# An attention and sign-weight block on one core: where a division is done, and how projection work is laid between attention steps

## The chip, the cores and the metric

The kernel runs on one core of one Trainium2 chip. Such a core has a matrix engine (TensorE, PE in the profile; its weight loads are listed apart as PEld), a vector engine (VectorE, DVE), a scalar engine (ScalarE, ACT), a general engine (GpSimd, POOL) and a queue engine that only issues transfers (SyncE, SP). POOL issues transfers as well as computing. Each engine works through its own list of instructions in order; semaphores hold an instruction until what it needs is there. The metric is the device time of one execution in microseconds (us), and the median of several executions is compared.

## The reference

The input is x of shape (2, 1024, 1024): two batches of 1024 tokens of 1024 channels. After a layer norm, xn goes into two branches whose results are added to x:

```
x = x + attention(xn) + binary_linear(xn)
attention:
  q, k, v = split(clip(xn @ Wqkv.T, -8, 8))
  q, k = layer_norm(q) * w + b, layer_norm(k) * w + b     # over 1024 channels
  32 heads of 32 channels
  scores = q k^T / sqrt(32) + slope[h] * (key - query), causal
  softmax over keys, times v; then @ Wout.T
binary_linear:
  W = mean(|W_real|, axis=1) * sign(W_real);  xn @ W.T + bias
```

All inputs and outputs are float32.

## The kernel before

**Projections.** Each of q, k, v and the output projection is a product of 1024x1024 blocks done with seven half-size products instead of eight (function `seven`, in the order of `ORDER`: 11, 21, t2, t3, t4, t1, 22). One of the seven is a group: four contraction chunks into one bank of PSUM, eight matmul instructions of 512 columns in the trace (each float32 product is two passes). A pair of token tiles (256 tokens) takes seven groups. `combine` folds the seven results on DVE and ACT. q and k rows are then layer-normed and transposed by `to_channels`, and stored to DRAM. The generator `pieces` hands out all of this as small pieces in order: k, q, v of the first batch, k, q, v of the second, then the sign-weight product (`binary_linear`), then the output projection (`output`). A yield gives a planner's cost: ONE = 0.915 for one chunk of a group, SHORT = 1.03 for four matmuls of the sign-weight product, TURN = 0.55 for four transposes.

**Attention.** Work is cut into 32 blocks (batch, half of the queries `qb`, group `g` of four heads). Per block there are first scores (`first_scores`, queries on partitions, DVE takes the row maxima straight out of PSUM, L1025) and second scores (`second_scores`, keys on partitions, the maxima brought in as three bfloat16 rows, L1081; DVE adds the causal mask on diagonal tiles, L1100; ACT takes the exponential out of PSUM into `pT`, L1109). `weigh_values` multiplies `pT` by the values (L1149); POOL adds up the `pT` tiles (L1138) for the softmax denominators. `divide` brings the denominators together with eight matmuls (`den`, L1168), ACT takes ln and exp(-1 x ln) (L1176, L1177), POOL multiplies (L1182, for the very last block DVE, L1180) and issues the store to DRAM (L1183). A matrix of 128 x 512 scores per head fills one of seven PSUM banks of the pool `ps_s`; the banks are handed out in turn, so a new tile waits until the tile seven allocations back has been read.

**The order of the steps.** The loop over n (L1228) is written out by hand. Step n holds, in this order: the first scores of unit n; when a block has closed, the start of its `shifts`; when a block's values were finished in the step before, its `divide`; a first `fill`; the values of unit n-10; the second scores of unit n-9 (LAG is 9); a second `fill`. There are 144 units and so steps 0 to 154. `fill(time)` draws pieces until its planned time is used up and carries an overdraft to the next call in `left["time"]`; in one of the two fills of a step the `sides` (layer norms, transposes, sign preparation) move on too. `middle` is 81. In steps below 81 a step's free time is `share` (8.08) less what attention is planned to take: 7.03 in steps 0 to 8, 4.63 in steps 10 to 80. BEFORE = 0.4 of it goes into the first fill and 0.6 into the second. From step 81 on there is only the second fill, with `each` = 3.69 and `whole=True`, by which the call goes on until the group that it has begun is finished. After the last step, `fill(float("inf"))` runs what is left.

**Start.** `projected("k", 0)` loads and norms token tiles 0 and 1, `turn_x` transposes a tile in two halves of four 128x128 transposes, and the first group follows. The last operation of `spread` (L501) is one ACT instruction over all 1024 channels, in place.

**End.** The last two pairs of token tiles of the output projection (14 groups) need the last block's division: `output` returns None until it is done, and then a `fill` stops and its balance is set to zero.

**Queues.** SP issues the weight loads (`load_weights`, into a ring of 28 tiles), the loads of keys, queries and values (L930, L934, L943), `load_pair` (L557), `prefetch` (L844) and the residual copies (L660). POOL issues the stores of intermediate results.

Of the kernel before, what the change touches and what calls it, by code (L numbers as in the profile page):

```python
# [8 lines left out]
FP = mybir.dt.float32  # L9
FR = mybir.dt.float32r  # L10
BF = mybir.dt.bfloat16
AF = mybir.ActivationFunctionType
ALU = mybir.AluOpType
# [12 lines left out]
def parallel_block_kernel(  # L26
# [36 lines left out]
    nc = tc.nc  # L63
    B, S, D = x.shape
    P = 128
    NT = S // P
    NC = D // P
    HALF = 512
# [7 lines left out]


    ONE, SHORT, TURN = 0.915, 1.03, 0.55
    BEFORE = 0.4
    PART, FOLD, SWITCH = 0.95 / 512, 0.3 / 512, 0.1  # L80
    QK_SCALE = HEAD_DIM ** (-0.5)
    slopes = [2.0 ** (-(h + 1) * ALIBI_BIAS_MAX / N_HEADS) for h in range(N_HEADS)]
# [6 lines left out]
    work = ctx.enter_context(tc.tile_pool(name="work", bufs=2))  # L89
# [117 lines left out]
    def half(n):  # L207
        return slice(n * HALF, (n + 1) * HALF)
# [127 lines left out]
    def advance_sides():  # L336
        time = 0.0
        for s in list(sides):
            cost = next(s, None)
            if cost is None:  # L340
                sides.remove(s)
            else:
                time += cost
        return time
# [10 lines left out]
    def score_bank(name):  # L355
        return ps_s.tile([P, HALF], FP, tag="s", name=name)
# [7 lines left out]
    kd, qd, vd, od, xd = ({} for _ in range(5))  # L364
# [29 lines left out]
    held = [False]  # L394
# [88 lines left out]
    def spread(src, stats, what):  # L483

        mv = small.tile([P, 2], FP, tag="mv", name=f"mv_{what}")
        nc.vector.bn_aggr(mv, stats.rearrange("p n s -> p (n s)"))
        if what[:2] != "x0":
            yield 0.0
        rstd = small.tile([P, 1], FP, tag="rstd", name=f"rstd_{what}")
        nc.scalar.activation(rstd, mv[:, 1:2], AF.Ln, bias=eps_t)  # L490
        nc.scalar.activation(rstd, rstd, AF.Exp, scale=-0.5)
        yield 0.0

        mean, var = mv[:, 0:1], mv[:, 1:2]
        t = small.tile([P, 1], FP, tag="newton", name=f"newton_{what}")
        nc.vector.tensor_scalar(var, var, EPS, -0.5, ALU.add, ALU.mult)
        nc.vector.tensor_scalar(t, rstd, var, rstd, ALU.mult, ALU.mult)
        nc.vector.tensor_scalar(rstd, t, 1.5, rstd, ALU.add, ALU.mult)
        nc.vector.tensor_scalar(t, mean, -1.0, rstd, ALU.mult, ALU.mult)
        yield 0.0  # L500
        nc.scalar.activation(src, src, AF.Identity, bias=t, scale=rstd)  # L501

    def transposed(src, c0, what):
        ps = ps_s.tile([P, 4, P], FP, tag="s", name=f"tr_{what}_{c0}")
# [312 lines left out]
    blocks = [(b, qb, g) for b in range(B) for qb in range(NQB) for g in range(NC)]  # L817
# [75 lines left out]
    def pieces():  # L893
        for b in range(B):
            yield from keys_or_queries("k", b)
            yield from keys_or_queries("q", b)
            yield from values(b)
        yield from binary_linear()
        yield from output()

    left = {"pieces": pieces(), "time": 0.0, "owed": 0.0}

    def fill(time, whole=False, sides_too=True):

        left["time"] += time
        while left["time"] > 0.0 or (whole and held[0]):
            cost = next(left["pieces"], None)
            if cost is None:  # L910
                left["time"] = 0.0
                break
            left["owed"] += 0.5
            left["time"] -= cost
            if sides_too and left["owed"] >= 1.0:
                left["owed"] -= 1.0
                left["time"] -= advance_sides()

    def fill_until(what):
        while what not in done:  # L920
            left["time"] = 0.0
            fill(0.01)
# [5 lines left out]
    def load_keys(b, qb, g):  # L928
        q = group.tile([P, HALF], FP, tag="q", name=f"qg_{b}_{qb}_{g}", bufs=6)
        nc.sync.dma_start(q, qd[b][g][:, half(qb)])  # L930
        k = []
        for n in range(qb + 1):
            k.append(group.tile([P, HALF], FP, tag="k", name=f"kg_{b}_{qb}_{g}_{n}", bufs=6))
            nc.sync.dma_start(k[n], kd[b][g][:, half(n)])  # L934
        st["q", b, qb, g], st["k", b, qb, g] = q, k
# [13 lines left out]
    def open_block(*block):  # L949
        st[("mx",) + block] = small.tile(  # L950
            [P, G, NQ], FP, tag="mx", name="mx_{}_{}_{}".format(*block), bufs=3
        )
# [210 lines left out]
    def divide(b, qb, g):  # L1163

        ps = score_bank(f"den_{b}_{g}_{qb}")
        total = st.pop(("sum", b, qb, g))
        for j in range(G):
            nc.tensor.matmul(  # L1168
                ps[32 * j : 32 * j + 32, :],
                ones,  # L1170
                total[j],
                start=True,
                stop=True,
            )
        inv = work.tile([P, HALF], FP, tag="inv", name=f"inv_{b}_{g}_{qb}", bufs=1)
        nc.scalar.activation(inv, ps, AF.Ln)  # L1176
        nc.scalar.activation(inv, inv, AF.Exp, scale=-1.0)  # L1177
        ot = st["ot", b, qb, g]
        if (b, qb, g) == blocks[-1]:
            nc.vector.tensor_tensor(ot, ot, inv, ALU.mult)  # L1180
        else:
            nc.gpsimd.tensor_tensor(ot, ot, inv, ALU.mult)  # L1182
            nc.gpsimd.dma_start(od[b][g][:, half(qb)], ot)  # L1183
        done.add(("o", b, qb, g))


# [30 lines left out]
    def short_lead(block):  # L1217

        return block[1] == 1 and block[2] == 0
# [3 lines left out]
    for n in range(3):  # L1223
        if n in opens:
            load_keys(*opens[n])
    fill(proj - AHEAD * ONE)
    chains = []
    for n in range(steps + 1):  # L1228
        if n + 3 in opens and not short_lead(opens[n + 3]):
            fill_until(("q", opens[n + 3][0]))  # L1230
            load_keys(*opens[n + 3])
        if n + 2 in weighs:
            block = weighs[n + 2]
            fill_until(("v", block[0]))
            load_values(*block)
        if n in opens:
            open_block(*opens[n])
        if n < len(first):
            first_scores(first[n])
        closing = shifts(*closes[n]) if n in closes else None  # L1240
        if closing:
            next(closing)
        m = n - LAG
        if m - 2 in ends:
            divide(*ends[m - 2])
        free = max(share - time_of(n), 0.0)
        if n < middle:
            fill(free * BEFORE, sides_too=False)
        if 0 <= m - 1 < len(second):
            weigh_values(second[m - 1], ends.get(m - 1))  # L1250
        if 0 <= m < len(second):
            second_scores(second[m])
        for c in chains:
            next(c, None)
        chains = [closing] if closing else []
        if n + 2 in opens and short_lead(opens[n + 2]):
            fill_until(("q", opens[n + 2][0]))
            load_keys(*opens[n + 2])
        if n < middle:
            fill(free * (1.0 - BEFORE))  # L1260
        else:
            fill(each, whole=True)
    fill(float("inf"))
# [51 lines left out]
```

## Time and profile before

| what | value |
|---|---|
| median of 3 executions | 1578.15 us (1576.8 to 1581.82) |
| the profiled execution | 1580.05 us, its span 1578.3 us |
| granted TensorE clock, mean | 0.992 |
| POOL: multiplication in `divide`, L1182 | 31 x 1273 ns, and 114.3 us of waiting before them |
| POOL: issue of its store, L1183 | 31 x 619 ns |
| ACT: ln out of PSUM, L1176; exp, L1177 | 32 x 601 ns; 32 x 630 ns |
| ACT: last step of the norm of x, L501 | 16 x 1269 ns |
| step of the second half with a whole group, 1365.95 to 1372.94 us | 6.99 us |

How to read it: a page of the profile gives busy time per engine and groups of instructions with their mean duration; the chain of waits and the list of waits say what ended an engine's idle time; the timeline lists instructions in order of time, with start and duration. A matmul that waits in the middle of a group shows as a group that lasts long, not as idle time of PE. So how long PE really spends on a group is read from the start of the group to the start of whatever PE does next.

### The profile page before, as it was taken

Reading aid. Unit: us, or ns where it says so; the run is one execution under the profiler, and the core shown is the slowest. Engines: PE = TensorE matmul, PEld = TensorE weight load, DVE = VectorE, ACT = ScalarE, POOL = GpSimd, SP = SyncE. Lnnn points to the kernel's source line nnn. Section 1 sums busy time; section 2 is a strip of 40 time slices with the busy share of each in tenths; the row PEclk is TensorE's granted clock in tenths of the full one; section 3 lists DMA queues with packets and bytes.
Section 4 is the critical chain, followed back from the end, with each engine's and each line's share of the span. In section 5 each row is a group of like instructions: output and inputs, shape, how many; then the busy total and the mean of one; then the engine's idle time right before and its main releaser. Section 6 shows DMA issues by size and latency. Waiting matters only on the chain.

```text
span 1578.3 us, 25307 instructions
## 1 busy us (share of the span) xinstructions
PE 1553.1 (98%) x8452; PEld 682.3 (43%) x8452; DVE 909.5 (58%) x2602; ACT 688.5 (44%) x1425; POOL 998.8 (63%) x1306
## 2 busy tenths in 40 slices
PE   7999999999999999999999999999999999999998
PEld 3444444444444434333333344555555433333343
DVE  7745353766676666666666555656555556555232
ACT  2553341114665645545542374545444434434420
POOL 4473071024675566676566599887798988778841
PEclk9999999999999999999999999999899999999999
DMA  7776364592323655558742377656565831233232
GB/s 290 295 254 261 100 206 151 185 324 74 107 95 112 224 191 182 131 129 253 249 159 94 115 250 221 140 130 136 134 147 97 225 87 39 77 81 74 57 78 53
DMA packets 116466, 244.94 MB, mean 155 GB/s; under 512 B 10544, under 2 KB 50992, under 8 KB 113008
## 3 DMA queue, kind: packets, MB, share of 16 engines
q1 hardware_dynamic: 88752, 145.01, 27.8%
q0 software_dynamic: 27584, 98.32, 24.0%
q8 instruction: 67, 1.10, 0.3%
q14 instruction: 63, 0.52, 0.1%
HBM read 155.47 MB, written 107.74 MB: 167 GB/s over the span
## 4 chain that ended last, share of the span: by engine, by line
PE 65%; DVE 1%; POOL 1%; issue 1%; ACT 1%; DMA 0%; POOLq 0%; DVEq 0%; ACTq 0%
PE s L1006 9%; PE s L1067 9%; PE o L1149 8%; PE mm_f L793 8%; PE mm_o_t L402 7%; PE mm_o L402 5%; PE mm_q_t L402 4%; PE mm_v_t L402 4%; PE mm_q L402 3%; PE mm_v L402 3%; PE den L1168 2%; PE s L1081 2%; PE mm_k_t L402 1%; PE mm_k L402 0%; PE tr_q L506 0%
## 5 line engine op out<-in xcount | busy, mean ns | idle before, releaser
L1138 POOL TENSOR_TENSOR pT<-pT,pT 128x512 f32<-128x512 f32 (+3 forms) x628 | 579.9, 983 | 101.8 <-ACT pT L1109 100.9
L1109 ACT ACTIVATE pT<-s,kpos 128x512 f32<-128x512 f32 (+3 forms) x768 | 378.2, 590 | 464.5 <-DVE s L1100 274.1
L1025 DVE CUSTOM_DVE_ANT_0 sumss<-s,rel 128x512 f32<-128x512 f32 (+2 forms) x284 | 179.1, 631 | 112.4 <-PE s L1006 79.3
L1006 PE MATMUL s<-kg,qg 32*128 32x512 f32 (+3 forms) x1536 | 197.3, 523 | 0.7 <-ACT kT L570 0.6
L1067 PE MATMUL s<-qg,kg 32*128 32x512 f32 (+3 forms) x1536 | 176.7, 525 | 1.3 <-DVE mx L1025 1.3
L1149 PE MATMUL o<-pT,vg 128*32 128x512 f32 (+3 forms) x1536 | 155.3, 499 | 0.0
L793 PE MATMUL mm_f<-sg,hl 128*128 128x512 f32 x512 | 128.6, 403 | 2.1 <-DVE mx L1025 2.1
L1006 PEld LDWEIGHTS s<-kg,qg 32*128 32x128 f32 x1536 | 80.0, 183 | 110.4 <-issue 44.8
L1100 DVE TENSOR_TENSOR s<-s,behind 128x256 f32<-128x256 f32 (+1 forms) x320 | 96.9, 371 | 48.1 <-PE s L1081 47.9
L402 PE MATMUL mm_o_t<-w_o_t,ot 128*128 128x512 f32 x256 | 116.6, 602 | 0.0
L1067 PEld LDWEIGHTS s<-qg,kg 32*128 32x128 f32 x1536 | 71.7, 185 | 101.4 <-issue 56.3
L1182 POOL TENSOR_TENSOR ot<-ot,inv 128x512 f32<-128x512 f32 x31 | 39.5, 1273 | 114.3 <-ACT inv L1177 114.3
L402 PE MATMUL mm_k_t<-w_k_t,xT 128*128 128x512 f32 x224 | 110.7, 614 | 0.5 <-DVE mx L1025 0.4
L793 PEld LDWEIGHTS mm_f<-sg,hl 128*128 128x128 f32 x512 | 94.7, 190 | 34.4 <-DVE mx L1025 10.6
L402 PE MATMUL mm_q_t<-w_q_t,xp 128*128 128x512 f32 x224 | 108.2, 605 | 0.0
L402 PE MATMUL mm_v_t<-w_v_t,xp 128*128 128x512 f32 x224 | 106.3, 606 | 0.1
L402 PE MATMUL mm_k<-w_k,xT 128*128 128x512 f32 x192 | 91.4, 616 | 0.9 <-DVE mx L1025 0.7
L402 PE MATMUL mm_v<-w_v,xp 128*128 128x512 f32 x192 | 89.6, 604 | 0.0
L1149 PEld LDWEIGHTS o<-pT,vg 128*32 128x32 f32 x1536 | 37.3, 109 | 119.1 <-issue 102.8
L402 PE MATMUL mm_q<-w_q,xp 128*128 128x512 f32 x192 | 88.7, 603 | 0.0
L402 PE MATMUL mm_o<-w_o,ot 128*128 128x512 f32 x192 | 87.5, 602 | 0.1
L1025 DVE CUSTOM_DVE_ANT_0 umss<-s,rel 128x512 f32<-128x512 f32 x100 | 69.2, 692 | 26.1 <-PE s L1006 15.3
(222 smaller groups left out, 2009.0 us busy)
## 6 DMA issues: line engine op xcount, KB each, us to landing
xp<-xd SPq DMA_DIRECT2D x16, 1792.0 KB, 8.3
kg<-kd SPq DMA_DIRECT2D x48, 256.0 KB, 5.0
vg<-vd SPq DMA_DIRECT2D x48, 256.0 KB, 7.9
wd_ot<-in_wout_t_dram POOLq DMA_DIRECT2D x11, 1024.0 KB, 9.4
xd<-xT POOLq DMA_DIRECT2D x8, 1280.0 KB, 5.3
x<-in_x_dram SPq DMA_DIRECT2D x16, 512.0 KB, 6.3
kd<-kT POOLq DMA_DIRECT2D x16, 512.0 KB, 4.1
qd<-qT POOLq DMA_DIRECT2D x16, 512.0 KB, 4.2
```

What stands on the lines that cost most here:

```text
L402: nc.tensor.matmul(ps, pr[:, FACTOR[block], c, :], W[what, block, c], start=(c == 0), stop=(c == NI - 1),)
L793: nc.tensor.matmul(ps, hl[c // NI][:, m % 2, c % NI, :].bitcast(FR), sg[n, c], start=(m == 0), stop=(m == 2 * NC - 1),)
L1006: nc.tensor.matmul(banks[j][:, c0 : c0 + n], q[r, tokens(i - block[1] * NQ)], k[r, :n], start=True, stop=True,)
L1025: nc.vector.tensor_tensor_reduce(out=sums[:, :n], in0=banks[j][:, c0 : c0 + n], in1=rel[:, o0 : o0 + n], scale=1.0, scalar=m if opened els ...
L1067: nc.tensor.matmul(banks[j][:, c0:c1], k[r, tokens(kt % NQ)], q[r, q0:], start=(c0 == 0), stop=False,)
L1081: nc.tensor.matmul(banks[j][:, c0:c1], ones_b[r, :], rows[r, q0:], start=False, stop=(c1 == HALF or (block, kt, q0) == unit[-1]),)
L1100: nc.vector.tensor_tensor(at, at, mask, ALU.add)
L1109: nc.scalar.activation(pT[:, c0:c1], banks[j][:, c0:c1], AF.Exp, bias=kpos[:, h, a : a + 1], scale=slopes[h],)
L1138: eng.tensor_tensor(part_sum, part_sum, pT[j], ALU.add)
L1149: nc.tensor.matmul(po[32 * j : 32 * j + 32, q0:], v[:, kt % NQ, 32 * j : 32 * j + 32], pT[j], start=(kt == 0), stop=(last is not None and ...
L1168: nc.tensor.matmul(ps[32 * j : 32 * j + 32, :], ones, total[j], start=True, stop=True,)
L1182: nc.gpsimd.tensor_tensor(ot, ot, inv, ALU.mult)
```

## The change

Four edits.

1. In `divide`, ln and exp work in place in the PSUM bank of `den`, the tile `inv` is gone, DVE does the multiplication in all blocks with that bank as an operand, and SP issues the store.
2. In `spread`, the last ACT instruction for token tiles 0 and 1 of the first batch is done as two instructions over 512 channels each.
3. The first fill of a step below 81 gets what is over 4.0 of the free time (LATER), and the second gets the rest, up to 4.0. In steps 10 to 80 that is 0.63 and 4.0 instead of 1.85 and 2.78.
4. A call of `fill` with `whole=True` draws at least one piece, whatever the balance.

```diff
-    BEFORE = 0.4
+    LATER = 4.0
...
-        nc.scalar.activation(src, src, AF.Identity, bias=t, scale=rstd)
+        parts = (half(0), half(1)) if what in ("x0_0", "x0_1") else (slice(0, D),)
+        for at in parts:
+            nc.scalar.activation(
+                src[:, at], src[:, at], AF.Identity, bias=t, scale=rstd
+            )
...
         left["time"] += time
-        while left["time"] > 0.0 or (whole and held[0]):
+        none = whole
+        while left["time"] > 0.0 or none or (whole and held[0]):
+            none = False
             cost = next(left["pieces"], None)
...
-        inv = work.tile([P, HALF], FP, tag="inv", name=f"inv_{b}_{g}_{qb}", bufs=1)
-        nc.scalar.activation(inv, ps, AF.Ln)
-        nc.scalar.activation(inv, inv, AF.Exp, scale=-1.0)
+        nc.scalar.activation(ps, ps, AF.Ln)
+        nc.scalar.activation(ps, ps, AF.Exp, scale=-1.0)
         ot = st["ot", b, qb, g]
-        if (b, qb, g) == blocks[-1]:
-            nc.vector.tensor_tensor(ot, ot, inv, ALU.mult)
-        else:
-            nc.gpsimd.tensor_tensor(ot, ot, inv, ALU.mult)
-            nc.gpsimd.dma_start(od[b][g][:, half(qb)], ot)
+        nc.vector.tensor_tensor(ot, ps, ot, ALU.mult)
+        if (b, qb, g) != blocks[-1]:
+            nc.sync.dma_start(od[b][g][:, half(qb)], ot)
         done.add(("o", b, qb, g))
...
         if n < middle:
-            fill(free * BEFORE, sides_too=False)
+            fill(max(free - LATER, 0.0), sides_too=False)
...
         if n < middle:
-            fill(free * (1.0 - BEFORE))
+            fill(min(free, LATER))
         else:
             fill(each, whole=True)
```

## The prediction

> **What bounds the kernel now.** I read the page first: PE is busy for 98% of the span and every other engine for 64% or less.
>
> ```profile
> span 1578.3 us, 25307 instructions
> PE 1553.1 (98%) x8452; PEld 682.3 (43%) x8452; DVE 909.5 (58%) x2602; ACT 688.5 (44%) x1425; POOL 998.8 (63%) x1306
> ```
>
> PE is the bound, so only three things can pay: PE starting sooner, waiting less, or switching less between kinds of work. Waits inside a group count as busy, so I went to the timeline next (start, duration, engine and line, operation) and measured each group from its start to the start of PE's next work. A quiet step of the second half:
>
> ```profile
> 1365.95 1.14 PE L1006 MATMUL s<-kg,qg 32*128 32x512 f32 x8
> ...
> 1369.31 3.70 PE L402 MATMUL mm_o_t<-w_o_t,ot 128*128 128x512 f32 x8
> ...
> 1372.94 1.14 PE L1006 MATMUL s<-kg,qg 32*128 32x512 f32 x8
> ```
>
> First scores take 1.07 (to 1367.02, where the values start), and no first fill exists here; 3.63 of product after the second scores is enough for the next first scores to start unheld. Now a step while the second batch's keys are projected:
>
> ```profile
> 495.58 3.03 ACT L1109 ACTIVATE pT<-s,kpos 128x384 f32<-128x384 f32 x8 [4.64 <-DVE s L1100]
> ...
> 497.75 2.03 PE L1006 MATMUL s<-kg,qg 32*128 32x512 f32 x8
> ...
> 499.71 0.70 PE L402 MATMUL mm_k_t<-w_k_t,xT 128*128 128x512 f32 x1
> ```
>
> First scores take 1.96 here, because the exponentials of the step before still hold two of the banks until 498.6; 2.7 us of product lay between. Over steps 9 to 80 the first scores are held in 27 steps, by 22.7 us in all. In the second half the worst places are steps that have no product at all:
>
> ```profile
> 1125.17 5.55 PE L1006 MATMUL s<-kg,qg 32*128 32x512 f32 x8
> ...
> 1127.76 3.03 ACT L1109 ACTIVATE pT<-s,kpos 128x256 f32<-128x256 f32 x8 [3.93 <-DVE s L1100]
> ...
> 1134.11 5.64 PE L793 MATMUL mm_f<-sg,hl 128*128 128x512 f32 x16
> ```
>
> The second scores end at 1125.17 and the next first scores follow at once; they are held for 4.4 us, and then the sixteen sign-weight matmuls, 3.85 elsewhere, take 5.57. The view of windows says why (columns: window, length, busy time of PE, PEld, DVE, ACT, POOL with counts, then the granted clock):
>
> ```profile
> 1132.00:1136.00 4.00, 4.00 (x17) 1.85 (x14) 0.89 (x4) 1.91 (x4) 1.65 (x8) 0.50 0.23 46
> ```
>
> After a hold of some 4 us the clock is halved for a while. Last, the end of attention, and two lines of the list of waits (waiter, releaser, us in total, times, longest):
>
> ```profile
> 1509.34 1.15 PE L1067 MATMUL s<-qg,kg 32*128 32x384 f32 x16
> ...
> 1514.19 1.37 DVE L1138 TENSOR_TENSOR pT<-pT,pT 128x384 f32<-128x384 f32 x5 [0.17 <-ACT pT L1109]
> ...
> 1518.90 1.06 PE L1168 MATMUL den<-pT,ones 128*32 128x512 f32 x8
> ```
>
> ```profile
> POOL ot L1182 <- ACT inv L1177: 114.3, 26, 9.8
> ...
> PEld s L1067 <- DVE mx L1025: 29.5, 51, 1.4
> ```
>
> **A product at least in each step.** From step 81 a step is granted 3.686 but a sign-weight group costs 4 x 1.03 = 4.12, so the balance falls by 0.434 a step and after 8 or 9 steps the grant doesn't lift it above zero. That gives three steps without a product: 89, 98 and 108 (second scores followed by first scores at 1052.45, 1125.17 and 1203.03). What they cost: steps 89 and 90 together take 18.05, where the same groups unheld take 3.27 + 1.07 + 0.88 + 1.40 + 0.97 + 0.33 + 3.85 = 11.8, so 6.3; step 99 takes 14.51 instead of 7.24, so 7.3; step 109 takes 9.64 instead of 8.49, so 1.1. With the edit all three get a group: **-14.7**.
>
> What is late next: three groups are used up sooner. Before, 29 sign-weight and 42 free output groups last from step 81 to 153 with three gaps (the 42nd behind the last division at 1519.9); now 71 groups fill steps 81 to 151, and steps 152 and 153 have none. There the last second scores (1509.34 in the trace, 1.29 long) are followed by their values (1.0) and the last division, whose sums DVE ends at 1515.56, 6.2 us after those scores began. PE has 2.3 of work in 6.2: a hold of 3.95, which 8.3 us of product and values covered before. Holds of 3.6 (step 90) and 4.4 (step 99) were each followed by half clock, for some 6.8 and 10.2 us by windows over them (0.56 over 1055 to 1062; 0.82, 0.50, 0.50, 0.82 from 1125 to 1141), and a shorter one near 355 by 3.4. Half of the middle one is 3.4 of lost time; ends 0 and 5.1. Together **+7.3** (4 to 9). Behind the division the sixth output group needs nothing new: the first group of the last pairs reads only channels stored long before, 3.4 us against the 3.2 that ln, exp and product took (1518.90 to 1522.09), and only the fourth chunk of the second needs the result.
>
> The Trainium skill, "TensorE: Matmul & The Clock Gate", section "What's actually happening", says that an idle window of about 3.4 us halves the clock and that about as long a busy one restores it; by that the end's half clock would cost 1.7, an estimate from that page, and the sum below would be 1547. The trace agrees on the halving, but its spells were one to three such windows long, so I stay with the row.
>
> **Length of the fills.** The total is the same (4.63 in steps 10 to 80), so the same pieces run. With 0.63 before and 4.0 after, and 0.915 a piece, the carry gives mostly one piece before and four after, and in about a third of the steps none and five, where it was two and three. The stretch from second scores to next first scores grows by 0.86 to 1.7 us. A hold can shrink by no more than itself, nor by more than the exponentials come sooner relative to it: in 17 held steps behind four row maxima (0.69 + 0.08, done some 3.9 after first scores begin) the cut by 1.2 each, or the whole where smaller, is 12.5 of 14.0; in the others, behind eight short maxima, which end 5 us or more after, the mask waits for DVE anyway, and I take half of 8.7. **-16.8**; ends -8 (the first kind alone by 0.6) and -22.7.
>
> Each run of products between attention work pays about 0.19 beside its matmuls (x6 takes 2.77, x4 1.91: 0.43 a matmul and 0.19 once). A third of some 71 steps lose one run: **-5** (-3 to -7). The cost side: second scores now come up to 1.2 us sooner after the first scores whose banks they take over. Weight loads for them already wait 29.5 us for the maxima, while PE is still busy; in the second half, with no first fill at all, second scores take 0.96, unheld. So 0, with up to +7 (0.1 a step) as upper end. The values keep the same distance to their exponentials.
>
> **Division.** POOL loses 31 x 1.27, 31 x 0.62 of issuing and 114.3 us of waiting in order, behind which stood its sums and shifts. PE waited for POOL only a little: transposes of shifts, 0.23 free, took longer by 3.7 us in the second half and 1.9 before. I take **-1** (0 to -5). DVE gets 32 x 0.69 (the row of `u_o` from PSUM, 692 ns), one of them there before. In order, the product stands behind the maxima of its step and ahead of the masks. In 24 of 30 divisions with maxima in the step exp ended before the last maximum; in the others it would hold DVE for up to 2.2, 5.5 us in all. Masks and with them exponentials come 0.7 later in those steps, mostly into slack: **+1** (0 to +10; all on the path would be 27). Ln and exp in place: no row has PSUM to PSUM; copies out of PSUM take 0.59 and exp between SBUF 0.63, so +-0.05, nothing. The bank is held until the product, 2 to 3 us longer; it is needed seven allocations on, a step later: 0.
>
> The store waits on SP for DVE's product. In 30 of 31 cases SP had issued the load ahead of it before that (0.29 late in one), so it goes out 0.9 to 4 us sooner than POOL did, and the next block's copy into `ot` (two waits, 8.8 us) gains at no cost to PE. Loads behind it on SP can no longer run ahead: up to 19 us later (queries at 864.9, used near 904, landing in 6.4; the last sign weight at 939.0 by 4.7, landed at 945.0, used at 953.9): 0.
>
> **Start.** ACT's 1.24 us instruction at 7.17 becomes two of about 0.63. The first transposes begin at 7.9 instead of 8.55, ACT's copy and the first product (10.31) come earlier by the same: **-0.55** (0 if weight loads, which PEld awaits at 13.03, take over; -0.65 at most).
>
> **Sum:** -14.7 + 7.3 - 16.8 - 5 - 1 + 1 - 0.55 = -29.75. The profiled execution took 1580.05 (span 1578.3 and 1.75 around it), so 1550.3; it stands 1.9 above the median of the three, and from the median the sum is 1548.4, say **1548**.
>
> **Rivals.** (a) The holds stay: DVE and ACT, not the place of the second scores, set when banks come free while keys are projected (DVE 70% and ACT 64% busy from 410 to 470). Against it: there DVE waits for PE before the masks (1.9 us at 495). Then 1548.4 + 16.8 = **1565**. (b) The end takes the product's gain back: 14.7 instead of 7.3 lost if the half clock comes twice: **1556**. (c) Slower: second scores are pinned by DVE's reading of the first scores' banks, so what moves behind them only turns into a wait ahead of them. If each of 71 steps loses 0.86 there and the holds stay, 1565 + 61 = **1626**; it decides at 29.75 / 71 = 0.42 a step. For it: the 29.5 us of waiting weight loads. Against it: unheld second scores in the quiet steps. (d) The least piece never acts, since all is carried anyway: 1548.4 + 14.7 - 7.3 = 1556; against it stand the three bare steps, which the carry explains to the step.
>
> **Chances.** The forecast as worked 0.58, (a) 0.17, (b) and (d) 0.10, (c) 0.09, several small losses that leave no change 0.06. Differences under 0.3% (5 us) a measurement of this kernel can't tell from none. Faster 0.85, same 0.05, slower 0.10. The range goes from 1535 (all holds gone, no half clock at the end) to 1567 (past (a)).
>
> **What would show it.** Right: no two scores without product after 1000 us; a bare stretch of some 4 us ahead of the last `den`, half clock behind it; 14 groups after that `den`, not 15; `den` and its product on DVE without long waits; first scores near 1.07 in steps 11 to 80; POOL near 960 us busy (998.8 - 39.5). Wrong: L1067 or L1081 groups that grow in steps 10 to 80, or DVE standing before its product.

## The result, and the profile after

The changed kernel takes 1575.72 us (median of 20 executions, 1569.74 to 1578.78) against 1579.56 us for the kernel before (20 executions, 1576.61 to 1583.57): a ratio of 0.997 with an interval of 0.9959 to 0.9981. It is 4 to 5 us faster (3.8 by the medians, 4.7 by the ratio); the forecast was 30, and 1575.72 lies above the range of 1535 to 1567. The profiled execution took 1578.76 us, its span 1577.0, 1.3 us less than the span before. It lies 3 us above the median, so the trace is that of one of the longer executions. A gain of this size says little about which edits worked, so the places come first.

The head of the page of the changed kernel, and from its list of groups (busy us, mean ns | idle before) the attention scores that answer to L1006 and L1067 before:

```profile
span 1577.0 us, 25397 instructions
...
PE 1554.0 (99%) x8452; PEld 684.3 (43%) x8452; DVE 928.5 (59%) x2633; ACT 687.0 (44%) x1427; POOL 939.5 (60%) x1244
...
L1073 PE MATMUL s<-qg,kg 32*128 32x512 f32 (+3 forms) x1536 | 199.9, 526 | 1.9 <-DVE mx L1031 1.7
L1012 PE MATMUL s<-kg,qg 32*128 32x512 f32 (+3 forms) x1536 | 173.0, 521 | 0.2
```

The two lines of the kernel before:

```profile
L1006 PE MATMUL s<-kg,qg 32*128 32x512 f32 (+3 forms) x1536 | 197.3, 523 | 0.7 <-ACT kT L570 0.6
L1067 PE MATMUL s<-qg,kg 32*128 32x512 f32 (+3 forms) x1536 | 176.7, 525 | 1.3 <-DVE mx L1025 1.3
```

First scores (L1012) last 24.3 us less, second scores (L1073) 23.2 us more. A matmul's mean time hardly moved; the groups are longer because matmuls in them wait. PE's idle time shows nothing of it.

To place this I took every group of every step from the timeline, from its start to the start of PE's next work, and call *held* what goes beyond its unheld length (first scores 1.08, second scores with their row matmuls 1.30, values 1.0, product 0.43 a matmul and 0.2 a run). In us:

| steps | | before | changed |
|---|---|---|---|
| 9 to 29 | length of these steps | 202.4 | 210.0 |
| | first scores held | 15.6 | 6.0 |
| | second scores held | 6.5 | 18.6 |
| | products longer (half clock) | 1.6 | 8.0 |
| 30 to 80 | length | 431.3 | 434.6 |
| | first scores held | 7.2 | 2.2 |
| | second scores held | 2.4 | 13.8 |
| 81 to 142 | length | 469.1 | 465.1 |
| | first scores held | 10.7 | 0.1 |
| | second scores held | 4.6 | 5.3 |

Steps 9 to 80, where the lengths of the fills act, became 10.9 us *longer*. Part of that belongs to this execution: its granted clock over 350 to 551 us is 0.93, against 0.99 before, while the kernel with the lengths alone (below), which has the same fills there, shows 0.97 and takes 639.8 us for steps 9 to 80 (633.7 before, 644.6 here). Steps 81 to 142, where the least product acts, became 3.9 shorter although three groups more (3 x 3.63 = 10.9) now stand in them, moved forward from the end.

A held step of the changed kernel, step 58, from the timeline (start, duration, engine and line, operation, in brackets the idle time before it and what ended it):

```profile
796.99 1.15 PE L1012 MATMUL s<-kg,qg 32*128 32x384 f32 x16
...
798.07 1.06 PE L1155 MATMUL o<-pT,vg 128*32 128x512 f32 x8
...
799.07 2.02 PE L1073 MATMUL s<-qg,kg 32*128 32x512 f32 x7
...
799.99 0.35 DVE L1031 CUSTOM_DVE_ANT_0 s<-s,rel,mx 128x128 f32<-128x128 f32 x1
800.26 0.08 DVE L1031 DVE_READ_ACCUMULATOR2_ANT mx<- 128x1 f32 x1
800.40 0.18 PEld L1073 LDWEIGHTS s<-qg,kg 32*128 32x128 f32 x1 [0.87 <-DVE mx L1031]
...
800.93 0.59 PE L1073 MATMUL s<-qg,kg 32*128 32x512 f32 x1
```

First scores, values, second scores, with no product ahead of the second scores. Seven matmuls go through; the last weight load stands until DVE has read the second head's maximum out of its bank (800.34), and 2.60 us pass instead of 1.30. In the list of waits the total of this wait grew; one line of the changed kernel, which had 29.5 us in 51 waits before:

```profile
PEld s L1073 <- DVE mx L1031: 41.9, 74, 1.5
```

The end, from the timeline of the changed kernel, and the clock over it from the view of windows (window, length, busy time of PE, PEld, DVE, ACT, POOL with counts, granted clock, DMA share, GB/s):

```profile
1516.19 1.15 PE L1073 MATMUL s<-qg,kg 32*128 32x384 f32 x16
...
1518.81 3.24 PE L1155 MATMUL o<-pT,vg 128*32 128x384 f32 x16 [1.25 <-ACT pT L1115]
...
1522.41 1.62 PE L1174 MATMUL den<-pT,ones 128*32 128x512 f32 x8 [0.36 <-DVE pT L1144]
```

```profile
1516.00:1526.00 10.00, 8.39 (x57) 3.26 (x54) 5.86 (x13) 4.77 (x11) 7.99 (x9) 1.00 1.00 269
1526.00:1536.00 10.00, 10.00 (x24) 4.38 (x23) 3.51 (x9) 0.58 (x1) 0.96 (x2) 1.00 0.14 28
```

The two steps without product are there, held by 4.5 us (1.3 in the second scores, 2.6 in the values, 0.6 in the division), and the clock stays whole.

### The profile page after: what moved, and what is told of

It is laid out like the page before. It is cut to its first block, busy times and chain, and to the rows that moved or that the text cites. A ratio compares the mean times of both kernels' runs of the same rounds, so it can differ in the third digit from the quotient of the medians.

```text
span 1577.0 us, 25397 instructions
## 1 busy us (share of the span) xinstructions
PE 1554.0 (99%) x8452; PEld 684.3 (43%) x8452; DVE 928.5 (59%) x2633; ACT 687.0 (44%) x1427; POOL 939.5 (60%) x1244
## 4 chain that ended last, share of the span: by engine, by line
PE 90%; DVE 4%; DMA 2%; POOL 1%; issue 1%; ACT 1%; SPq 0%; POOLq 0%; DVEq 0%; ACTq 0%
PE s L1073 10%; PE s L1012 9%; PE o L1155 8%; PE mm_f L797 7%; PE mm_q_t L402 7%; PE mm_v_t L402 7%; PE mm_o_t L402 7%; PE mm_k_t L402 6%; PE mm_q L402 5%; PE mm_v L402 5%; PE mm_o L402 5%; PE mm_k L402 4%; PE s L1087 2%; PE den L1174 2%; DMA vd<-vraw 1%
## 5 line engine op out<-in xcount | busy, mean ns | idle before, releaser
L1073 PE MATMUL s<-qg,kg 32*128 32x512 f32 (+3 forms) x1536 | 199.9, 526 | 1.9 <-DVE mx L1031 1.7
L1012 PE MATMUL s<-kg,qg 32*128 32x512 f32 (+3 forms) x1536 | 173.0, 521 | 0.2
L1073 PEld LDWEIGHTS s<-qg,kg 32*128 32x128 f32 x1536 | 82.1, 185 | 113.7 <-issue 49.6
L1012 PEld LDWEIGHTS s<-kg,qg 32*128 32x128 f32 x1536 | 69.0, 184 | 106.0 <-issue 55.0
L402 PE MATMUL mm_k<-w_k,xT 128*128 128x512 f32 x192 | 96.8, 648 | 0.3 <-ACT xT L537 0.3
L1087 PE MATMUL s<-rows,ones_b 3*128 3x512 bf16 (+3 forms) x768 | 74.6, 326 | 0.0
```

Source lines behind the costliest of these rows:

```text
L402: nc.tensor.matmul(ps, pr[:, FACTOR[block], c, :], W[what, block, c], start=(c == 0), stop=(c == NI - 1),)
L1012: nc.tensor.matmul(banks[j][:, c0 : c0 + n], q[r, tokens(i - block[1] * NQ)], k[r, :n], start=True, stop=True,)
L1073: nc.tensor.matmul(banks[j][:, c0:c1], k[r, tokens(kt % NQ)], q[r, q0:], start=(c0 == 0), stop=False,)
L1087: nc.tensor.matmul(banks[j][:, c0:c1], ones_b[r, :], rows[r, q0:], start=False, stop=(c1 == HALF or (block, kt, q0) == unit[-1]),)
```

## The experiments

Line numbers move by up to six between the kernels. The kernel before was run again beside each group of kernels, with medians of 1579.4 to 1581.3, so I compare ratios.

### The edits apart

**All but the lengths of the fills**: the changed kernel with edit 3 undone.

```diff
-    LATER = 4.0
+    BEFORE = 0.4
...
-            fill(max(free - LATER, 0.0), sides_too=False)
+            fill(free * BEFORE, sides_too=False)
...
-            fill(min(free, LATER))
+            fill(free * (1.0 - BEFORE))
```

> The changed kernel with the fills as before (0.4 of the free time ahead, 0.6 behind). Theory 1: the length of the fills is what lost 11 us between steps 9 and 80 in the changed kernel, because the second scores came too early for their banks. Then steps 9 to 80 take 632 to 635 us here, second scores are held there by 9 us or less, first scores by some 20 again, and the time is 11 us under the changed kernel's, near 1565, or 0.9% under the kernel before. Theory 2: the division did it (its bank is held through ln, exp and product, and DVE waits for ACT). Then steps 9 to 80 still take 640 us or more and the time stays near 1576.

**The lengths alone**: the kernel before with the same lines the other way round.

> The kernel before with the fills of the changed one alone. Theory 1: steps 9 to 80 take 643 to 646 us (633.7 before), second scores held by some 30 us there, the three bare steps stay, and the time is some 11 us over the kernel before, near 1590, or 0.7% slower. Theory 2: steps 9 to 80 stay near 634, the time within 3 us of the kernel before.

**The least product alone**: the kernel before with edit 4.

```diff
-        while left["time"] > 0.0 or (whole and held[0]):
+        none = whole
+        while left["time"] > 0.0 or none or (whole and held[0]):
+            none = False
```

> The kernel before with at least one piece a step from step 81 on, alone. Theory 1: no step without a product, 14 us gained between 1000 and 1210 us, some 4.5 given back in a hold ahead of the last division: 9 to 10 us under the kernel before, near 1569, ratio 0.994. Theory 2 has no other number for it, only that it then explains the whole gain of the changed kernel and the division has to lose some 6 us.

**The division alone**: the kernel before with edit 1.

> The kernel before with the division on DVE out of PSUM and its store on SP, alone. Theory 1: within 3 us of the kernel before (POOL some 40 us less busy, DVE 20 more, both beside PE). Theory 2: 6 to 11 us over it, with second scores held behind divisions before step 81.

Measured, against the kernel before:

| kernel | median us | ratio | interval |
|---|---|---|---|
| changed kernel | 1575.72 | 0.997 | 0.9959 to 0.9981 |
| all but the lengths | 1571.32 | 0.9945 | 0.9931 to 0.9959 |
| lengths alone | 1590.61 | 1.0061 | 1.0044 to 1.0077 |
| least product alone | 1578.21 | 0.9991 | 0.9981 to 1.0 |
| division alone | 1580.38 | 0.9995 | 0.9985 to 1.0006 |

The lengths of the fills lose time wherever they are: 9.6 us alone, some 4 on top of the others. In the traces steps 9 to 80 take 635.2 us without edit 3 and 639.8 with it alone (633.7 before); 632 to 635 and 643 to 646 were expected, and the time without edit 3 came out at 1571.3, not near the expected 1565. With the old lengths, second scores of steps 30 to 80 are held 0.8 us and first scores 6.9; with the lengths alone 16.6 and 1.7. So the hold did not go; it moved from the first scores to the second and grew there. The page of the kernel without edit 3 turns the two lines round again:

```profile
L1012 PE MATMUL s<-kg,qg 32*128 32x512 f32 (+3 forms) x1536 | 187.6, 524 | 0.7 <-ACT kT L574 0.6
L1073 PE MATMUL s<-qg,kg 32*128 32x512 f32 (+3 forms) x1536 | 176.9, 521 | 0.9 <-DVE mx L1031 0.9
```

The division alone is worth nothing that can be measured, as forecast. The number expected of the least product alone missed: it gives 1.4 us alone, but edits 1, 2 and 4 together give 8.7. That is taken up below.

### Why second scores are held: the banks

In the built program, `ps_s` has seven banks of PSUM, handed out in turn to scores, products and the rest. In step 58 the first scores have banks 1, 4, 6 and 2, and the second scores 0, 3, 1 and 4. Bank 5 holds a product that the step's boundary cut: a group of four pieces of which one came in the step before. So six banks rotate, and the fourth second score needs the bank of the *second* first score, the third that of the first. In step 120, where groups are whole, all seven rotate (first scores 3, 6, 1, 4; second scores 2, 5, 0, 3), and only the fourth second score has to wait, for the *first* maximum. So a new tile waits for the one seven allocations back only while no group stands half finished; otherwise it is the one six back. Two experiments on that.

**Six banks**: the changed kernel with one bank less in the rotation.

```diff
-    ps_s = ctx.enter_context(tc.tile_pool(name="ps_s", bufs=7, space=bass.MemoryType.PSUM))
+    ps_s = ctx.enter_context(tc.tile_pool(name="ps_s", bufs=6, space=bass.MemoryType.PSUM))
```

> The changed kernel with six banks of PSUM in the rotation instead of seven, everywhere. In the second half, where groups are whole and second scores are held 5 us in 62 steps, this puts the fourth bank of second scores on one that the second head's maxima read last, as a cut group does in the first half. Theory 3: held time of second scores in steps 81 to 142 rises to 20 to 45 us (0.3 to 0.7 a step), the time to 1595 or more; in steps 30 to 80 it rises too, since a cut group now leaves five. Rival 4 (the number of banks doesn't matter, the order does): steps 81 to 142 stay below 10 us, the time below 1583.

Measured: 1684.04 us (one execution). Second scores of steps 81 to 142 are held 53.9 us in all 62 steps, 0.87 a step, where the changed kernel has 5.3; in steps 30 to 80 it is 47.6 instead of 13.8. The amount is above what was expected, the sign is not in doubt. From its page and its list of waits:

```profile
L1073 PE MATMUL s<-qg,kg 32*128 32x512 f32 (+3 forms) x1536 | 287.8, 526 | 5.5 <-DVE mx L1031 3.5
```

```profile
PEld s L1073 <- DVE mx L1031: 111.9, 189, 1.5
```

The same order of work that is unheld in the second half with seven banks is held in every step with six.

**Whole groups**: no fill behind the first scores, and the one behind the second scores run to the end of a group, in the first half too.

```diff
-        if n < middle:
-            fill(max(free - LATER, 0.0), sides_too=False)
...
-            fill(min(free, LATER))
+            fill(free, whole=True)
```

> The changed kernel with no fill behind the first scores in the first half, and the one behind the second scores run to the end of a whole group, so that no half-finished product stands in a bank of PSUM when a step begins (the second half has always been filled so). Theory 3, a cut group keeps a bank: in steps 30 to 80 the changed kernel's second scores are held 13.8 us beyond their 1.3, since their fourth bank is one that the second head's maxima still read. With all seven banks in rotation this falls to 4 or less, first scores stay within 3 of their 1.08, and step 81 begins some 10 to 14 us sooner than the changed kernel's 994.5; the time is 1560 to 1566, below that of all but the length of the fills (1571). Rival 4, order alone: second scores that stand with no fill behind first scores and values are early for their maxima with any number of banks; then the holds of steps 30 to 80 stay at 12 or more, and the time is within 4 us of the changed kernel's 1576. In steps 9 to 29, where layer norms of the second half of the tokens stand on DVE ahead of maxima, both leave holds of 8 or more.

Measured: 1600.31 us (1594.46 to 1607.06), ratio 1.0128 (1.0102 to 1.0154): wrong by far. The steps split in two. In 57 to 76, the values' projection, second scores are held 3.8 us in twenty steps that all lack a product ahead of them; the changed kernel has 4.7 in its seven such steps. That is 0.19 a step instead of 0.67, so there the kept bank was most of the hold. In 30 to 56, the queries' projection, the hold is 25.3 us. Its timeline in step 42 shows what stands ahead of the maxima:

```profile
662.34 1.14 PE L1012 MATMUL s<-kg,qg 32*128 32x512 f32 x8
662.45 0.69 DVE L433 TENSOR_TENSOR u_q<-mm_q_t,u_q 128x512 f32<-128x512 f32 x1 [1.55 <-PE mm_q_t L402]
...
663.05 0.69 DVE L433 TENSOR_TENSOR mm_q_t<-mm_q_t,u_q 128x512 f32<-128x512 f32 x1
...
663.78 0.69 DVE L444 TENSOR_SCALAR qraw<-mm_q_t 128x512 f32<-128x512 f32 x1
...
664.39 1.28 DVE L480 BATCH_NORM_STATS2 stats_q<-qraw 128x6 f32<-128x512 f32 x2
...
665.82 0.64 DVE L1031 CUSTOM_DVE_ANT_0 sumss<-s,rel 128x512 f32<-128x512 f32 x1
...
666.52 0.18 PEld L1073 LDWEIGHTS s<-qg,kg 32*128 32x128 f32 x1 [1.71 <-DVE mx L1031]
```

The group that ends with the step before hands DVE three passes out of PSUM and the statistics of a layer norm, all of it in order ahead of the maxima: the first maximum begins 3.5 us after the first scores, not 1.2 us as in step 58. In this step a whole group frees a bank but brings its norm to the worst place. So banks are not all: the second scores wait for a maximum, the number of banks decides for which, and DVE's work at the step's start decides when it is there.

**Thin statistics**: the changed kernel with the statistics of three norms (second-quarter tokens, second batch's keys and queries) over 32 columns of each half instead of 512, so most of the mean and variance sums of these norms are left out.

```diff
-            nc.vector.bn_stats(stats[:, n, :], src[:, half(n)])
+            few = 32 if what[:2] in ("x1", "k1", "q1") else HALF
+            nc.vector.bn_stats(stats[:, n, :], src[:, n * HALF : n * HALF + few])
```

> The changed kernel with the statistics of three layer norms (tokens of the second quarter of the image, keys and queries of the second batch) taken over 32 columns of each half instead of 512: that part of the computation is left out, and DVE has some 0.6 to 1.2 us less for each of its four instructions a tile in steps 9 to 29. It asks which work stands ahead of the maxima there. Theory 3 with DVE late for the norms: second scores' holds in steps 9 to 29 fall from 18.6 to 10 or less, the products' extra time (half clock) from 8.0 to 3 or less, and step 30 comes 10 us sooner; steps 30 to 80, which have none of these statistics, keep their 13.8 within 3. Rival: the holds of steps 9 to 29 are of the same kind as later ones (a bank kept by a cut group), 21 steps x 0.27 = 6, plus the exponentials'; then they stay above 14.

Measured: 1566.87 us (one execution). Steps 9 to 29 take 197.8 instead of 210.0 us, their second scores are held 11.2 instead of 18.6 and their products 4.1 longer instead of 8.0; steps 30 to 80 stay at 14.5 (13.8). Second scores and products stayed just above the 10 and 3 expected; most of the fall lies in three steps: 9 (second scores 5.71 to 3.41 us), 13 (4.97 to 3.51) and 19 (3.58 to 1.58). How much of this is the norms is less sure than it looks, because part of a step's length is the half clock, and that varies between executions (below); step 19, which takes 3.58 to 4.10 in the changed kernel, with the lengths alone, with one piece ahead and with that and the even end, is the clear one. The kernel with the lengths alone, also with whole statistics, takes 202.2 us for steps 9 to 29 and holds second scores 16.1 there, so the fall in the hold is surer than the one in the length. Step 26 hardly moved (5.23 to 4.81), so it has another cause that I didn't find.

**One piece ahead**: the changed kernel with exactly one piece (two matmuls) behind the first scores in each step of the first half that has product to give.

```diff
-        if n < middle:
-            fill(max(free - LATER, 0.0), sides_too=False)
+        if n < middle and free > ONE:
+            carried, left["time"] = left["time"], 0.0
+            fill(0.01, sides_too=False)
+            left["time"] += carried - 0.01
...
-            fill(min(free, LATER))
+            fill(free)
```

> The changed kernel with exactly one piece of product (two matmuls) behind the first scores in each step of the first half that has product to give, and the rest behind the second scores; the changed kernel has one in most steps and none in about a quarter. In its steps 30 to 76 the second scores are held 8.1 us in the 11 steps with no piece ahead of them and 2.4 us in the 36 with one. Theory 3 (without a piece ahead, the fourth bank of second scores isn't free; one piece covers it): holds of second scores in steps 30 to 76 fall to about 3, those of first scores stay below 1.5, and these steps take 390 to 393 us instead of 397.9 (394.4 with the old lengths, two fifths ahead). Steps 9 to 29, where norms stand on DVE ahead of the maxima, keep holds of 15 to 30. The time is 1567 to 1573. If the holds don't hang on the piece but on what DVE and ACT have to do in those steps, they stay where they are, 9 or more in steps 30 to 76, and the time stays within 3 us of 1576.

Measured: 1568.48 us (1564.9 to 1576.38), ratio 0.9931 (0.9907 to 0.9954). Steps 30 to 76 by the product that stands ahead of the second scores (us held in all, second scores of a step and the first scores of the next):

| kernel | pieces ahead | steps | second scores | next first scores | length of steps 30 to 76 |
|---|---|---|---|---|---|
| changed | none | 11 | 8.1 | 0.4 | 397.9 (with the next row) |
| changed | one | 36 | 2.4 | 0.4 | |
| one piece ahead | one | 47 | 3.4 | 0.8 | 393.1 |
| old lengths | two | 47 | 0.6 | 4.8 | 394.4 |

One piece is nearly enough for both sides. Its step 58, where the changed kernel took 2.60 for the second scores, takes 1.55:

```profile
785.47 1.15 PE L1012 MATMUL s<-kg,qg 32*128 32x384 f32 x16
...
786.55 1.13 PE L402 MATMUL mm_v_t<-w_v_t,xp 128*128 128x512 f32 x2
...
787.61 1.06 PE L1155 MATMUL o<-pT,vg 128*32 128x512 f32 x8
...
788.60 1.40 PE L1073 MATMUL s<-qg,kg 32*128 32x512 f32 x8
```

So of the changed kernel's 13.8 us in steps 30 to 80, most belongs to the quarter of the steps in which the carry left no piece. Steps 9 to 29 keep 12.7, below the 15 to 30 expected.

**Whole groups where there are no norms**: the old lengths and the end of the next section, and in steps 57 to 76 whole groups behind the second scores.

```diff
+        late = 57 <= n < 77
-        if n < middle:
+        if n < middle and not late:
             fill(free * BEFORE, sides_too=False)
...
-        if n < middle:
+        if late:
+            fill(free, whole=True)
+        elif n < middle:
             fill(free * (1.0 - BEFORE))
```

> The kernel with the old lengths and the even end (1570.3), with one thing more: in steps 57 to 76, where the product is the values' projection and has no norms, all of it goes behind the second scores in whole groups. Theory 3 (whole groups keep no bank, and with no norms on DVE the maxima are early enough): these twenty steps take 163.7 us, as they did in the kernel with whole groups everywhere, instead of 167.0, and the time is 3 us less: 1567. Rival: the gain there came from elsewhere (the rest of that kernel was slower, with DVE and POOL behind); then they take 166 to 168 and the time is 1570.

Measured: 1567.58 us (1565.02 to 1573.12), ratio 0.9921 (0.9901 to 0.9941), but the twenty steps take 167.6 us, not 163.7 (167.0 without it). Second scores are held 4.5 there, where the old lengths don't hold them at all, and first scores 0.8 instead of 1.8. So the expected mechanism gives nothing. The 163.7 of the kernel with whole groups comes from less work lying in those steps: 192 product matmuls and 20 transposes there, 198 and 28 here. That its median is 2.7 below that of the next kernel is inside both intervals.

### The end

**An even end**: the old lengths, and 3.2 pieces of product a step in steps 144 to 153 instead of whole groups.

```diff
-        else:
+        elif n < len(first) or n >= steps:
             fill(each, whole=True)
+        else:
+            if n == len(first):
+                left["time"] = 0.0
+            fill(3.2 * ONE)
```

> The changed kernel with the old lengths of the fills (two fifths behind first scores), and in steps 144 to 153 an even 3.2 pieces of product a step, groups cut where they must, in place of whole groups to the due time, so that the last two steps of attention aren't bare. If the hold at the end is paid for the lack of a product there, the bare stretch ahead of the last denominators (4.5 us held in the changed kernel and in the kernel with the old lengths) shrinks below 1.5, and the time is 3 us below that of the old lengths (1571.3): 1568. If cut groups cost a bank there too, second scores of steps 144 to 153 are held by as much as is won, some 0.4 a step, and the time is 1571 to 1573.

Measured: 1570.31 us (1566.76 to 1571.89), ratio 0.9932 (0.9917 to 0.9946) against 0.9945 (0.9931 to 0.9959) without it: not told apart. In the trace the last second scores and the last `den` go unheld (1.30 and 1.00), but values are held 2.0 in four steps, the last of them taking 1.72 instead of 1.0. From step 143 to the end of the span it is 115.3 instead of 117.3 us: a gain of 2 of the 4.5.

**One piece ahead and the even end** together:

> One piece ahead in each step of the first half (1568.5 by itself) together with the even end, 3.2 pieces a step in steps 144 to 153 (115.2 us from step 143 to the end of the span, where whole groups take 117.3). If the two are independent, as their places are, the time is 2 us below the one piece alone: 1566.5, with held time of steps 9 to 142 as there. If the even end gives nothing by itself, 1568.5.

Measured: 1569.21 us (1566.04 to 1572.66), ratio 0.9933 (0.9917 to 0.995), the same as one piece alone (0.9931). The even end gives nothing that the median shows.

### Why the least product needs the division

**The store on POOL**: all but the lengths of the fills, with only the issue of the division's store given back to POOL.

```diff
-            nc.sync.dma_start(od[b][g][:, half(qb)], ot)
+            nc.gpsimd.dma_start(od[b][g][:, half(qb)], ot)
```

> The changed kernel with the old lengths, but the division's store is issued by POOL as before, behind VectorE's product. POOL is then rid of the product (31 x 1.27 us) but still waits in order for the end of the division before it goes on to its sums. It asks why a product at least in each step saved 1.4 us alone and 8.6 together with the division on VectorE. If the wait in order is what holds PE's transposes and products in the second half, this kernel keeps most of least-only's loss: held time of transposes, second scores and half clock in steps 81 to 142 of 12 us or more, steps 81 to 142 at 470 to 472, and 1575 to 1578. If POOL's busy time was it, steps 81 to 142 take 465 to 467 as with the store on SP, and the time is 1571 to 1573.

Measured: 1579.07 us (1575.72 to 1583.7), ratio 0.9985 (0.9974 to 0.9996). POOL no longer multiplies (958.5 us busy, 998.8 before), but the gain is gone, as with the least product alone: steps 81 to 142 take 471.1 us (471.6 there, 465.1 with the store on SP). So it is not POOL's product that matters but that POOL waits in order. Its list of waits:

```profile
POOL od L1186 <- DVE ot L1184: 149.5, 25, 11.7
POOL pT L1144 <- ACT pT L1115: 105.0, 56, 10.7
```

And what it does to PE in step 113, from the timeline:

```profile
1214.00 0.59 POOL L1186 DMA_DIRECT2D od<-ot  x1 [8.91 <-PE mm_f L797]
1214.60 7.72 POOL L1144 TENSOR_TENSOR pT<-pT,pT 128x256 f32<-128x256 f32 x8
1222.28 1.25 POOL L388 TENSOR_TENSOR ot<-ot 128x512 f32<-128x512 f32 x1
...
1242.96 0.21 POOL L1047 TENSOR_TENSOR sh<-mx,pos 128x16 f32<-128x16 f32 x1
...
1245.15 0.58 PE L1058 MATMUL trs<-ident_b,shift_b 128*128 128x128 bf16 x4 [3.90 <-POOL shift_b L1051]
...
1245.52 5.21 PE L402 MATMUL mm_o_t<-w_o_t,ot 128*128 128x512 f32 x8
```

POOL stood 8.91 us for the store, and behind it are its sums and additions, one after the other without a gap, so that the shifts come 5.2 us after the step's first scores. PE waits 3.90 for them and then runs eight matmuls in 5.21 us instead of 3.65, at a granted clock of 0.72 (1244 to 1250). With the store on SP the same transposes wait 0.65: there the sums that begin here at 1214.60, 23.2 us ahead of the step's first scores, begin 26.6 us ahead of them. Of these 3.4 us the issue itself is only 0.59; the rest is the wait. The step takes 12.84 us instead of 7.90, which is 4.9 of the 6.0 us that steps 81 to 142 lose; with the least product alone it takes 12.22.

In the kernel before, step 113 takes 7.41 us although POOL waits for the division there too. The order of POOL's work was another:

```profile
1231.80 0.76 POOL L1041 TENSOR_TENSOR sh<-mx,pos 128x16 f32<-128x16 f32 x1
...
1239.32 1.29 POOL L388 TENSOR_TENSOR ot<-ot 128x512 f32<-128x512 f32 x1
```

The shifts come 3.2 us ahead of the step's first scores (1235.04), and POOL's additions for the output projection (L388 to L392) stand behind them. With a product in each step the output's groups are drawn sooner, and eight of these additions, some 10 us, stand ahead of the shifts: in the changed kernel, with the least product alone, in all but the lengths and here. From then on a wait of POOL ahead of them reaches PE.

## Why the prediction was right and wrong

By the terms of the sum, from the two profiled spans (-1.3 us):

- **A product at least, -14.7: right, under a condition.** Steps 81 to 142 show -3.9 with 10.9 more product in them, so -14.8; the three bare steps are gone (step 90 took 14.78 us before, 8.51 now). But alone it gives only 8.4 there (471.6 - 10.9 - 469.1); the rest hangs on the division's store having left POOL, and most of it lies in step 113 (12.22 us alone, 7.86 in the changed kernel). One reading was short: step 109 was taken from 1203.50, but its first matmul stands at 1203.03, so it lost 1.6 and not 1.1.
- **The end, +7.3: place right, size off.** The two bare steps are where they were foretold, with 14 groups behind the last `den`. The hold is 4.5 (3.95 foretold); the 3.4 for half clock was too much: the clock stayed whole. The Trainium skill, "TensorE: Matmul & The Clock Gate", section "What's actually happening", gives about 3.4 us of idling for the halving. Here PE was idle in short pieces, none as long (1.25 us is the longest marked one), and no halving came, which fits, though no run tests it; the row of before that I went by was a hold of 4.4.
- **Length of fills, -16.8: right.** First scores' holds in steps 9 to 80 fell by 14.6. The runs of products: 2.4 less in steps 30 to 76 beside the holds (397.9 - 11.3 against 394.4 - 5.4), where -5 over 71 steps is -3.3.
- **The cost side, "So 0, with up to +7 (0.1 a step) as upper end": this is the step that failed.** Second scores' holds grew by 23.5 in steps 9 to 80, and the half clock behind them by 6.4: together 0.42 a step, just where rival (c) decides (0.42; that the two agree to the digit is chance). The kernel with the lengths alone repeats the first figure (23.9) and not the second (2.4), so the holds are firm, and how much half clock comes with them differs between executions. In the changed kernel the granted clock is 0.5 for a while in each of steps 9, 13, 19 and 26, whose second scores have the four longest holds (2.3 to 4.4 us). Second scores that grow in steps 10 to 80 were also the sign of being wrong that the prediction named, and rival (c) named the mechanism, with 0.09. I put it aside by the second half, where second scores go unheld with no product ahead of them. That evidence doesn't carry over: there groups are whole and seven banks rotate; in the first half a cut group keeps one, and with six banks the second half is held in all 62 steps. The 29.5 us of waiting weight loads, the row that spoke for it, was the better witness.
- **Division, 0: right alone** (0.9995). As foretold exp was rarely late: DVE waited 4.2 us before its product in two cases, and POOL fell to 939.5 busy (960 foretold; that figure left out the 31 x 0.62 us of issuing, and with the issue back on POOL it is 958.5). But I priced POOL's wait by what PE lost to it *before*, where the shifts stood ahead of POOL's additions. With the least product they stand behind them, and leaving the store on POOL costs 6.0 us in steps 81 to 142, where -1 was forecast for taking it away.
- **Start, -0.55: -0.3.** The halves take 0.76 each, not 0.63; first transposes begin at 8.24 (8.55).

The terms as measured, -14.8 + 4.5 - 14.6 - 2.4 + 23.5 + 6.4 - 0.3, make +2.3; transposes of steps 9 to 29 wait 1.4 less (0.2 for 1.6), and 1.9 is saved behind the last matmul (below), which makes -1.0 of the -1.3.

## What to carry to other kernels

When a fill is moved from one side of an engine's work to the other, price both sides alike: the hold that goes has a twin on the side that is laid bare. A quiet stretch of the same kernel is evidence only if it has the same buffers free; count the rotation, with half-finished groups in it, before reading it across. And price an engine's waiting in order against the order of its work in the kernel as it will be, not as it was: two edits worth 0 and 1.4 us apart were worth 8.7 together with the small one.

## What the runs showed of the hardware that was not expected

- The half clock makes equal instructions differ between executions. One piece ahead and the same with the even end issue the same work up to step 143, but steps 9 to 29 took 201.8 and 210.3 us. The windows over them, in this order:

```profile
350.00:551.00 201.00, 197.19 (x1258) 84.40 (x1250) 141.93 (x446) 116.69 (x258) 104.77 (x173) 0.98 0.38 127
```

```profile
350.00:551.00 201.00, 196.95 (x1211) 84.21 (x1204) 137.60 (x436) 110.97 (x247) 99.91 (x166) 0.94 0.35 118
```

  A granted clock of 0.98 against 0.94 over the same 201 us: 8 us of work less. Differences below that in these steps need medians, not one trace.
- The division's store lands in a median of 2.1 to 2.3 us when SP issues it and, by kernel, in 3.0 to 4.4 when POOL does (3.6 before the change; 4.3 with only the issue given back to POOL).
- From the last output group's start to the end of the span it is 10.21 us in every kernel where POOL issues the division's store and 8.1 to 8.3 in every one where SP does, with the same last instructions and a last transfer that lands in 2.0 us either way. What differs is POOL's closing instruction (DRAIN), after which the other engines finish: it lasts 7.88 us in the kernel before and 5.95 in the changed one. It lies inside what the time counts, since the time is 1.7 to 1.9 us above the span in every execution. The division alone has this too, without a gain in its median, whose interval is wide enough to hide it (0.9985 to 1.0006, where 1.9 us is 0.0012). Why the DRAIN is longer was not looked for.
